# A Mamba block between two ternary FFNs on one core: the first FFN of the chunks as a stream of its own

## The chip, the core and the metric

The kernel runs on one core of a Trainium2 chip. The metric is the device time in microseconds (us) of one execution. The core has five engines that work side by side, each with its own instruction queue, which it works through in order: TensorE (PE, matrix products; its weight loads are listed as PEld), VectorE (DVE), ScalarE (ACT), GpSimd (POOL) and SyncE (SP, which issues most of the DMA transfers).

## The reference

The input x is 4096 rows (time steps) of 1024 numbers, in float32. Three residual blocks follow each other:

```
x = x + 0.5 * ffn(layernorm(x))
x = x + mamba(layernorm(x))
x = x + 0.5 * ffn(layernorm(x))

ffn(x)   = x @ w.T * scale + bias       # w: the weight rounded to -1, 0, 1; both FFNs share it
mamba(x): u, z = x @ W_in.T             # 1024 columns each
          u  = silu(conv_b + 4-tap convolution of u in time)
          dt_r, B, C = u @ W_xproj.T    # 64, 16, 16 columns
          dt = softplus(dt_r @ W_dt.T + b_dt)
          h_t = exp(dt_t * A) * h_(t-1) + dt_t * B_t * u_t     # 16 states for each column
          y  = sum over the 16 states of h_t * C_t  +  u * Dskip
          return (y * silu(z)) @ W_out.T
```

The recurrence runs over all 4096 time steps, so its 16 states are carried from one piece of the input to the next.

## The kernel before

**Tiling.** The rows are cut into 16 chunks of 256 time steps (`NC` = 16, `T` = 256), each chunk into two tiles of 128 rows (`TT`). The columns lie on partitions, in 8 blocks of 128, and a chunk's recurrence runs in two halves of 4 blocks. So there are 32 half-chunks, each with 16 states.

**The stages of a chunk**, with the lines to look for in the profile:

- First FFN ("a"): statistics of the rows on ACT and POOL (`stats`, L393 to L407), normalizing on ACT (`normed`, L412), transposes on PE (L428), each transposed group cut into a high part by ACT (L456) and a low part by DVE (L458), products with the ternary weight on PE (L499: 64 for a chunk; for chunk 0 L530, as the weight's blocks come), bias added by a DMA from POOL's queue (L472), residual on DVE (L479).
- Norm and u: the same statistics and transposes again, copies by ACT (L585), products with the u half of `w_in` on PE (L616), first tap of the convolution on ACT (L550), three more on DVE (L560), silu on ACT (L566).
- `steps`: the products with `w_xp` (L640), copies (L645, L648), B and C written to DRAM and read back spread over all partitions (`bc`, by `fetch`), the dt products (L708) and softplus on ACT (L720).
- `gates`: the products with the z half of `w_in` (L675), copied by ACT (L689), silu (L694).
- Recurrence, for each half and each of the 16 states: ACT makes the decays (L913, four pieces for two scans), POOL the entering term h = u * B (L934, with a small addition of the carried state, L941), DVE two scans (L966), then the product with C (L981); PE sums the states by transposed products with an identity (L1019). For three of the 16 states (`PAIRED`) DVE adds two products first (L996).
- Gate with z on DVE (L1036), transposes (L750) and copies (L740), products with `w_out` on PE (L758), residual on DVE (L729), then the second FFN ("c"), which uses the same lines as the first, and the store.

**What sets the order.** No engine chooses at run time. While the program is built, a planner (`Streams`, with a cost for each operation written at each `yield`) plays the streams through and writes the instructions into one fixed order for each engine. A stream is a generator: it yields either what it wants next (an engine, a duration, an earliest time) or a condition to wait for, such as `when("z", c, 1)`. Of those that could start first, the one with the lowest rank goes; the ranks are the constants `DECAY, ENTER, ...` and `FFN_A, NORM, U_PART, ...`, and a stream may change its rank by yielding a number. So a wait in the source is a wait in the plan: it moves instructions in the queues, and is no instruction itself. The streams around the change are `front` (first FFN, norm and u, chunk after chunk), `gates` (z of a chunk, spawned by `front` when its u products are recorded), `back` (`w_out` and the second FFN), and those of the recurrence. How far a stream may get ahead is limited by the buffers: 7 row tiles `xs`, 2 `xts`, 2 each of `his` and `los`, 5 weight buffers, 4 `us`, 3 PSUM banks and 3 PSUM banks for decays.

Of the kernel before, what the change touches and what calls it, by code (L numbers as in the profile page):

```python
# [53 lines left out]
REACH = 160  # L54
ISSUE, ADDED = 950, 6000
SWITCH = 1300

LATE_P, LATE_X, LATE_D, LATE_N = 300, 300, 1200, 300
PAIRED = (0, 4, 8)

DECAY, ENTER, SUM, PREPARE, RECUR, GATE = 4, 3, 1, 0, 5, 0
FFN_A, NORM, U_PART, CONV, DELTA, OUT, FFN_C = 1, 1, 3, 2, 2, 2, 3

HOLD = 250, 0, 0, 500
Z = 2, 4


class Streams:
# [109 lines left out]
def macaron_mamba_kernel(  # L178
# [16 lines left out]
    NC = S // T  # L195
# [84 lines left out]
    ready = {}  # L280

    def when(*key):
        return (yield lambda: ready.get(key, INF))
# [60 lines left out]
    def streamed(load, n, ahead, rank):  # L344

        queue = []

        def fill():
            for i in range(n):
                yield lambda: 0 if len(queue) < ahead else INF  # L350
                w = yield from weights.take()
                load(i, w)
                queue.append((order.now + 5000, w))

        order.spawn(fill(), rank)
        return queue
# [209 lines left out]
            nc.scalar.activation(flat(u[c, half]), flat(u[c, half]), AF.Silu)  # L566
            ready["u", c, half] = end + REACH

    def front():
        for c in range(NC):  # L570
            yield FFN_A
            at = [3500, 5000]
            for t in range(TT if c else 0):
                x_tiles[c, t] = yield from xs.take()
                load_x(c, t)
                at[t] = order.now + 5000
            ends = yield from ffn(c, "a", FFN_A, at)
            yield NORM
            queue = streamed(u_weights, NB, 2, U_PART)
            ln, rows_, at = yield from stats(c, ends)  # L580
            xT = yield from xts.take()

            def keep(g, pt, at_):
                end = yield act(512, at_)
                nc.scalar.copy(  # L585
                    xT[:, 4 * g : 4 * g + 4, PAD + t * P : PAD + (t + 1) * P],
                    pt.rearrange("p (j q) -> p j q", q=P),
                )
                banks.put(pt, end)
                ends.append(end + REACH)  # L590

            xns = []
            for t in range(TT):
                xns.append((yield from normed(c, ln, rows_, t, at)))
            lns.put(ln, xns[-1][1])
            ends = []
            for t in range(TT):
                xn, at = xns[t]
                yield from transposed(xn, at, keep, NORM)
                while len(ends) < 2 * (t + 1):  # L600
                    yield lambda: ends[2 * t + 1] if len(ends) > 2 * t + 1 else INF

            end = yield pool(190)
            nc.gpsimd.tensor_copy(xT[:, :, PAD - KER + 1 : PAD], halo)
            at = max(end, ends[-1]) + REACH
            yield U_PART
            for blk in range(NB):
                if blk % HB == 0:
                    u[c, blk // HB] = yield from us.take()
                pp = yield from banks.take()  # L610
                w = yield from arrived(queue)
                wt = w.rearrange("p (k m) -> p k m", m=P)
                for k in range(NB):
                    if k % 4 == 0:
                        end = yield pe(8 * (KER - 1 + T) * FULL, at)
                    nc.tensor.matmul(  # L616
                        pp[:, : KER - 1 + T],
                        wt[:, k, :],
                        xT[:, k, PAD - KER + 1 : PAD + T],
                        start=(k == 0),  # L620
                        stop=(k == NB - 1),
                    )
                order.spawn(conv(c, blk, pp, end + REACH), CONV)
                weights.put(w, end)
                if blk == 0:
                    yield pool(190, at)
                    nc.gpsimd.tensor_copy(halo, xT[:, :, PAD + T - KER + 1 : PAD + T])
            order.spawn(gates(c, xT), Z[0])
            order.spawn(steps(c), DELTA)
# [27 lines left out]
        xds.put(xd[c], order.now + 2000)  # L657

    def gates(c, xT):
        queue = streamed(z_weights, NB, 2, Z[0])  # L660
        for half in range(2):
            yield Z[half]
            sz[c, half] = yield from szs.take()
            for b in range(0, HB, 2):
                pp = yield from banks.take()
                pp = pp.rearrange("p (t j) -> p t j", t=TT)
                for part_ in range(2):
                    w = yield from arrived(queue)
                    wt = w.rearrange("p (j k m) -> p j k m", j=2, m=P)
                    for t in range(TT):  # L670
                        end = yield pe(8 * T * FULL)
                        for i in range(HB):
                            k = part_ * HB + i

                            nc.tensor.matmul(  # L675
                                pp[:, t, :],
                                xT[:, k, PAD + t * P : PAD + (t + 1) * P],
                                wt[:, :, i, :],
                                start=(k == 0 and t == 0),
                                stop=(k == NB - 1),  # L680
                                skip_group_check=True,
                            )
                    weights.put(w, end)
                order.spawn(kept(c, half, b, pp, end + REACH), Z[half])
        xts.put(xT, end)
# [86 lines left out]
    def back():  # L772
        for c in range(NC - 1):
            yield OUT
            yT = []
            for half in range(2):
                if half:
                    yield from when("product", c, 1, 0)
                    queue = streamed(lambda i, w: out_weights(i // 2, i % 2, w), NB, 3, OUT)
                yT.append((yield from us.take()))  # L780
                yield from turned(c, half, yT[half])
            for q in range(D // QW):
                po = yield from banks.take()
                po = po.rearrange("p (t j) -> p t j", t=TT)
                for half in range(2):
                    w = yield from arrived(queue)
                    for t in range(TT):
                        end = yield pe(8 * QW * FULL)
                        by_w_out(po, yT[half], w, half, t)
                    weights.put(w, end)  # L790
                for t in range(TT):
                    order.spawn(mixed(c, q, t, po, end + REACH + LATE_X), OUT)
            for half in range(2):
                us.put(yT[half], end)
            for q in range(D // QW):
                end = yield from when("mixed", c, q, 1)
            yield FFN_C
            ends = yield from ffn(c, "c", FFN_C, [end, end])
            for t in range(TT):
                yield from give_out(c, t, slice(0, D), ends[t])  # L800
                xs.put(x_tiles.pop((c, t)), order.now + 0)
        yield from last(NC - 1)
# [74 lines left out]
    def fetch():  # L877
        for c, half, n in items:
            if n < 0:
                continue  # L880
            yield from when("bc", c)
            bc = yield from bcs.take()
            nc.sync.dma_start(
                flat(bc),
                bc_dram[c][n : n + 1].rearrange("o a b -> o (a b)").to_broadcast([P, 2 * T]),
            )
            coming[c, half, n] = bc
            ready["come", c, half, n] = order.now + 3000

    def skipping():  # L890
        for i, (c, half) in enumerate(halves):
# [33 lines left out]
    def enter():  # L925
        for c, half, n in items:
            if n < 0:
                continue
            yield from when("g", c, half)
            yield from when("come", c, half, n)  # L930
            bc = coming[c, half, n]
            h = yield from hs.take()
            end = yield pool(2300, 0, True)
            nc.gpsimd.tensor_tensor(  # L934
                h, u[c, half], bc[:, 0:1, :].to_broadcast([P, HB, T]), ALU.mult
            )
            if n + 1 == NST:
                us.put(u[c, half], end)
            yield from when("over", c, half)
            end = yield pool(140, 0, True)  # L940
            nc.gpsimd.tensor_tensor(h[:, :, 0], h[:, :, 0], over[c, half][:, :, n], ALU.add)  # L941
            entering[c, half, n] = h
            ready["enter", c, half, n] = end + REACH
            if n + 1 == NST:
                overs.put(over[c, half], end)

# [93 lines left out]
    for rank, gen in (  # L1040
        (0, ternary()),
        (0, halved()),
        (0, fetch()),
        (FFN_A, front()),
        (OUT, back()),
        (PREPARE, prepare()),
        (DECAY, decaying()),
# [72 lines left out]
```

## Time and profile before

| | us |
|---|---|
| median of 3 runs | 2622.4 (2619.84 to 2623.95) |
| the profiled execution | 2623.95 |
| its span, first to last instruction | 2622.2 |
| PE busy | 2473.1 |
| DVE busy | 2467.7 |
| ACT busy | 1953.2 |
| POOL busy | 1746.9 |
| DVE, scans (L966), 1024 of them | 1215.5 |
| DVE, products with C (L981), 512 | 694.0 |
| DVE, sums of two products (L996), 96 | 193.4 |
| first scan of chunk 0 starts at | 102.06 |
| first scan of chunk 1, of chunk 2, of chunk 3 | 268.31, 424.08, 579.1 |

The mean granted TensorE clock of the profiled execution is 0.98. A line of the timeline gives the start, the time from the first to the last end, the engine, the line and the operation, then the tile written, the tiles read and how many instructions were merged; in brackets the engine's idle time in front and what ended it. A float32 product on PE (such as L616, L675, L758) shows as two records.

### The profile page before, as it was taken

What the parts mean: (1) busy time and instruction counts of PE and PEld (TensorE: products, weight loads), DVE (VectorE), ACT (ScalarE), POOL (GpSimd) and SP (SyncE); (2) the same over time, 40 slices, a digit from 0 to 9 for tenths busy, and PEclk for the clock granted to TensorE, in tenths of its full rate; (3) what the DMA queues carried; (4) which work ended last, traced back from release to release, by engine and by line L of the source; (5) the groups of instructions that cost most, each with busy time, mean ns of one, the idle gap of its engine ahead of it and who ended that gap; (6) DMA issues with size and microseconds to landing.
All of it is one profiled execution on the core that took longest, in us unless ns stands there. A gap on an engine that the chain in (4) does not pass through costs nothing. (4 is left out here: it accounts for less than half of the span.)

```text
span 2622.2 us, 38817 instructions
## 1 busy us (share of the span) xinstructions
PE 2473.1 (94%) x13314; PEld 2118.7 (81%) x13314; DVE 2467.7 (94%) x2532; ACT 1953.2 (74%) x4084; POOL 1746.9 (67%) x1433
## 2 busy tenths in 40 slices
PE   5987999999999999999999999999999999999867
PEld 4776778888888888888888888888888888888756
DVE  5589999999999999999999999999999999999994
ACT  3678678787778878777797878779787887876652
POOL 0456767767676776767677676766767677776772
PEclk9999899999999999999999999999999999999988
DMA  5544445556544555555555544555654455554451
GB/s 166 156 134 129 149 128 174 158 176 181 165 150 141 177 165 176 160 169 151 156 164 181 173 152 153 160 166 163 188 165 146 141 175 159 177 175 151 122 156 37
DMA packets 218541, 410.68 MB, mean 157 GB/s; under 512 B 19172, under 2 KB 85860, under 8 KB 218344
## 3 DMA queue, kind: packets, MB, share of 16 engines
q1 hardware_dynamic: 209128, 374.65, 44.2%
q0 software_dynamic: 9216, 33.56, 6.9%
q8 instruction: 105, 1.72, 0.3%
q14 instruction: 92, 0.75, 0.1%
HBM read 390.82 MB, written 17.31 MB: 156 GB/s over the span
## 5 line engine op out<-in xcount | busy, mean ns | idle before, releaser
L934 POOL TENSOR_TENSOR h<-u,bc 128x1024 f32<-128x1024 f32 x512 | 1224.2, 2391 | 565.8 <-ACT da L913 257.7
L913 ACT ACTIVATE da<-dt,pr 128x255 f32<-128x255 f32 x2048 | 946.3, 474 | 432.1 <-DVE h L966 398.9
L966 DVE TENSOR_TENSOR_SCAN h<-da,h 128x512 f32<-128x512 f32 x1024 | 1215.5, 1206 | 31.8 <-ACT da L913 22.3
L981 DVE TENSOR_TENSOR p<-h,bc 128x1024 f32<-128x1024 f32 x512 | 694.0, 1355 | 0.1
L1019 PE MATMUL y<-ident,p 128*128 128x128 f32 x3584 | 480.7, 279 | 74.2 <-DVE p L981 59.9
L1019 PEld LDWEIGHTS y<-ident,p 128*128 128x128 f32 x3584 | 423.0, 144 | 136.8 <-DVE p L981 81.1
L616 PE MATMUL bank<-xT,weight 128*128 128x259 f32 x2048 | 477.4, 386 | 11.1 <-issue 7.6
L675 PE MATMUL bank<-weight,xT 128*128 128x256 f32 x2048 | 478.0, 382 | 2.9 <-DMA weight<-in_w_in 1.0
L758 PE MATMUL bank<-weight,u 128*128 128x256 f32 x2016 | 464.1, 380 | 2.9 <-DMA weight<-in_w_out 2.8
L616 PEld LDWEIGHTS bank<-xT,weight 128*128 128x128 f32 x2048 | 384.0, 192 | 73.5 <-issue 10.8
L675 PEld LDWEIGHTS bank<-weight,xT 128*128 128x128 f32 x2048 | 377.5, 191 | 51.8 <-DVE x L479 2.9
L758 PEld LDWEIGHTS bank<-weight,u 128*128 128x128 f32 x2016 | 373.9, 191 | 49.5 <-ACT da L913 2.5
L941 POOL TENSOR_TENSOR h<-h,over 128x4 f32<-128x4 f32 x512 | 343.0, 670 | 33.7
L499 PE MATMUL bank<-wf,lo 128*128 128x512 f32 x976 | 255.7, 404 | 3.8 <-DVE lo L458 3.7
L499 PE MATMUL bank<-wf,hi 128*128 128x512 f32 x976 | 244.7, 393 | 0.0
L499 PEld LDWEIGHTS bank<-wf,lo 128*128 128x128 f32 x976 | 181.1, 190 | 44.3 <-DVE lo L458 8.0
L560 DVE SCALAR_TENSOR_TENSOR u<-bank,pr,u 128x256 f32<-128x256 f32 x384 | 176.4, 467 | 38.7 <-ACT u L550 36.4
L499 PEld LDWEIGHTS bank<-wf,hi 128*128 128x128 f32 x976 | 181.5, 188 | 37.2 <-issue 0.3
L996 DVE TENSOR_TENSOR p<-p,p 128x1024 f32<-128x1024 f32 x96 | 193.4, 2014 | 0.0
L395 POOL TENSOR_SCALAR ln<-ln 128x1 f32<-128x1 f32 x96 | 35.8, 373 | 182.0 <-ACT tmp L393 178.7
L428 PE MATMUL bank<-ident,tmp 128*128 128x128 f32 x756 | 114.5, 285 | 33.1 <-ACT tmp L412 24.0
L428 PEld LDWEIGHTS bank<-ident,tmp 128*128 128x128 f32 x756 | 93.1, 146 | 52.8 <-ACT tmp L412 30.2
(98 smaller groups left out, 1966.5 us busy)
## 6 DMA issues: line engine op xcount, KB each, us to landing
bc<-bcd SPq DMA_DIRECT2D x512, 256.0 KB, 3.7
weight<-in_w_in SPq DMA_DIRECT2D x128, 512.0 KB, 4.6
weight<-in_w_in SPq DMA_DIRECT2D x256, 256.0 KB, 5.6
weight<-in_w_out SPq DMA_DIRECT2D x128, 512.0 KB, 4.1
x<-hbias POOLq DMA_DIRECT2D x64, 512.0 KB, 9.4
x<-in_x SPq DMA_DIRECT2D x32, 512.0 KB, 5.0
out<-x SPq DMA_DIRECT2D x30, 512.0 KB, 4.5
weight<-in_w_ffn SPq DMA_DIRECT2D x5, 512.0 KB, 7.2
```

Source lines behind the costliest of these rows:

```text
L428: nc.tensor.matmul(pt[:, j * P : (j + 1) * P], xn[:, k * P : (k + 1) * P], ident, start=(j == 0), stop=(j == 3), is_transpose=True, skip_g ...
L499: nc.tensor.matmul(pf, x[:, k, :], wf[:, k, cols], start=(x is lo and k == 0), stop=(x is hi and k == NB - 1),)
L616: nc.tensor.matmul(pp[:, : KER - 1 + T], wt[:, k, :], xT[:, k, PAD - KER + 1 : PAD + T], start=(k == 0), stop=(k == NB - 1),)
L675: nc.tensor.matmul(pp[:, t, :], xT[:, k, PAD + t * P : PAD + (t + 1) * P], wt[:, :, i, :], start=(k == 0 and t == 0), stop=(k == NB - 1), ...
L758: nc.tensor.matmul(po[:, t, :], yT[:, b, t * P : (t + 1) * P], wt[:, b, :], start=(half == 0 and t == 0 and b == 0), stop=(half == 1 and b ...
L913: nc.scalar.activation(da[:, i, 1:], dt[c, half][:, b, 1:], AF.Exp, scale=a_neg[:, half * HB + b, n : n + 1],)
L934: nc.gpsimd.tensor_tensor(h, u[c, half], bc[:, 0:1, :].to_broadcast([P, HB, T]), ALU.mult)
L941: nc.gpsimd.tensor_tensor(h[:, :, 0], h[:, :, 0], over[c, half][:, :, n], ALU.add)
L966: nc.vector.tensor_tensor_scan(rows_, flat(da), rows_, 0.0, ALU.mult, ALU.add)
L981: nc.vector.tensor_tensor(p, h, bc[:, 1:2, :].to_broadcast([P, HB, T]), ALU.mult)
L996: nc.vector.tensor_tensor(flat(p), flat(p), flat(q), ALU.add)
L1019: nc.tensor.matmul(y[t][:, b * P : (b + 1) * P], p[:, b, t * P : (t + 1) * P], ident, start=(first and b == 0), stop=(n == NST - 1 and b = ...
```

## The change

The first FFN leaves `front` and becomes a stream of its own, `first_ffns`, which keeps the rank `FFN_A` and goes from chunk to chunk as far as the buffers let it; `front` starts with rank `NORM` and waits for the FFN of its chunk. `front` takes its `xT` buffer ahead of the statistics and not behind them. `gates` waits in the plan until the z of the chunk in front is done (its half 1). Besides, some constants of the plan change: the rank of z's second half (4 to 5), the due time of a streamed weight (5000 to 3500 ns behind its issue), the moment from which the `w_out` loads of a chunk are issued (state 0 of half 1 to state 12), the due time of a broadcast B and C (3000 to 4000 ns), and 300 ns are added to the plan's due time of an entering term (`LATE_E`). The operations and their number are the same; the order on each engine is a new one.

```diff
-LATE_P, LATE_X, LATE_D, LATE_N = 300, 300, 1200, 300
+LATE_P, LATE_X, LATE_D, LATE_E, LATE_N = 300, 300, 1200, 300, 300
...
-Z = 2, 4
+Z = 2, 5
...
-                queue.append((order.now + 5000, w))
+                queue.append((order.now + 3500, w))
...
-    def front():
+    first = {}
+
+    def first_ffns():
         for c in range(NC):
-            yield FFN_A
             at = [3500, 5000]
             for t in range(TT if c else 0):
                 x_tiles[c, t] = yield from xs.take()
                 load_x(c, t)
                 at[t] = order.now + 5000
-            ends = yield from ffn(c, "a", FFN_A, at)
+            first[c] = yield from ffn(c, "a", FFN_A, at)
+            ready["ffn", c] = order.now
+
+    def front():
+        for c in range(NC):
             yield NORM
+            yield from when("ffn", c)
+            ends = first[c]
             queue = streamed(u_weights, NB, 2, U_PART)
+            xT = yield from xts.take()
             ln, rows_, at = yield from stats(c, ends)
-            xT = yield from xts.take()
...
     def gates(c, xT):
+        if c:
+            yield from when("z", c - 1, 1)
         queue = streamed(z_weights, NB, 2, Z[0])
...
-                    yield from when("product", c, 1, 0)
+                    yield from when("product", c, 1, 12)
...
-            ready["come", c, half, n] = order.now + 3000
+            ready["come", c, half, n] = order.now + 4000
...
-            ready["enter", c, half, n] = end + REACH
+            ready["enter", c, half, n] = end + REACH + LATE_E
...
-        (FFN_A, front()),
+        (FFN_A, first_ffns()),
+        (NORM, front()),
```

## The prediction

> **What bounds the kernel now.** First I read the page's totals and its forty slices:
>
> ```profile
> PE 2473.1 (94%) x13314; PEld 2118.7 (81%) x13314; DVE 2467.7 (94%) x2532; ACT 1953.2 (74%) x4084; POOL 1746.9 (67%) x1433
> ...
> DVE   5589999999999999999999999999999999999994
> ```
>
> VectorE (DVE) and TensorE (PE) are both full, except at the two ends. To see which of them sets the pace I cut the span at the first scan (L966) of chunks 0, 1, 2 and 3 (102.06, 268.31, 424.08 and 579.10 us in DVE's timeline) and asked for busy times by stretch; the columns are start:end, length, PE, PEld, DVE, ACT, POOL, PE clock, DMA share, GB/s:
>
> ```profile
> 0.00:102.06 102.06, 69.60 (x304) 57.74 (x305) 44.81 (x73) 47.56 (x77) 13.63 (x32) 0.93 0.52 168
> 102.06:268.31 166.25, 140.01 (x724) 118.14 (x722) 144.43 (x141) 130.61 (x264) 105.25 (x89) 0.91 0.43 128
> 268.31:424.08 155.77, 148.05 (x787) 126.69 (x788) 149.81 (x154) 112.32 (x239) 105.27 (x83) 0.96 0.54 162
> 424.08:579.10 155.02, 151.96 (x833) 130.60 (x833) 152.64 (x157) 121.64 (x256) 108.38 (x90) 1.00 0.54 164
> ```
>
> From chunk 2 on a chunk takes 155.0 us, DVE idles 2.4 of them and PE 3.1: DVE sets the pace. What is lost lies before the first scan (DVE idle 57.2 of 102.1 us), in chunk 0 (21.8) and in chunk 1 (6.0). DVE's waits, asked for chunk 0 and for chunk 1, begin with one line each (who waits for whom, us in total, times, longest):
>
> ```profile
> DVE h L966 <- ACT da L913: 11.3, 7, 6.3
> ...
> DVE h L966 <- POOL h L934: 4.1, 1, 4.1
> ```
>
> Scans wait for ScalarE's decays (ACT, L913), once for 6.3 us, and once for POOL's entering term (L934). So the total is: time of the first scan, plus DVE's remaining work, plus DVE's idle time after it.
>
> **What the change moves.** I compared the order of the instructions of both built programs, engine by engine. From the first scan of chunk 2 to that of chunk 14, DVE's and POOL's orders are the same, instruction for instruction; on PE and ACT one small group per chunk changes places (four transposed products L1019 behind eight products L758; one copy L689 behind two exponentials), and some loads on SP's queue. So the first FFN does not run ahead in the steady part any more than before. The change is chunks 0 and 1, and a little of chunk 15.
>
> **Part 1, the first scan.** PE gets, ahead of chunk 0's dt products (L708): the FFNs of chunks 1 and 2 (each 64 products at 8 in 1.82 us, 14.5, and 16 transposes L428 at 4 in 0.44, 1.8), chunk 1's norm transposes (1.8) and 16 more products for z (7.1 by "86.40 7.07 L675 x32", where one product is two records). Sum 41.5 us. Some of it falls into a gap of PE:
>
> ```profile
> 39.47 0.39 PE L530 MATMUL y<-wf,hi 128*128 128x512 f32 x1
> 48.72 3.67 PE L428 MATMUL bank<-ident,tmp 128*128 128x128 f32 x16 [8.87 <-ACT tmp L412]
> ```
>
> Chunk 1's transposes start at 39.8, its hi/lo chain (ACT 0.58, DVE 0.69 per group) lets the products start at 42.6; they end at 57.1. Chunk 0's norm transposes stand behind them; 2.7 us with their copies, so u (L616) starts at 59.8 instead of 52.26: +7.5. Into u go chunk 2's 16.3 us, and I add 1.2 for the hand-overs of the three PSUM banks; behind u stand 8.9 us of z and norm products more than before, of which 1.6 replace PE's wait for the silu at 84.59. L708 ends at 126.9 instead of 94.5 (+32.4). Behind it ACT now also has z's silu with its table (1.28 + 1.06), and DVE has six taps of chunk 1's convolution that wait for u's second block on PE: first scan at **136.8** instead of 102.1, **+34.7 us**. Bounds: 131.3, if PE never stalls (39.9 us plus 83.9 of ordered work gives 123.8, and the old 7.5 from L708's end to the scan); 139, if ACT holds up two of the convolutions by its L393/L397 of 1.0 to 1.2 each.
>
> A page speaks against this step. The Trainium skill, "ScalarE: Activation LUTs", section "What ACT_TABLE_LOAD costs", puts every switch at about 2.66 us, 1.28 of load and 1.38 of drain. In this trace the load takes 1.28 and the next activation starts 1.29 behind it (127.67, 128.97), with no drain of that size; with the page's figure the three switches ahead of the first scan would add an estimated 4.1 us, and I go by the row.
>
> **Part 2, what DVE has done by then.** Ahead of the first scan now stand 8 more L479 (0.66 apart: 5.3), 4 more L458 (0.61: 2.4) and 6 taps L560 (0.49: 2.9): **-10.7 us** that chunk 0 need not do. Net at this point: +24.0.
>
> **Part 3, chunk 0.** 21.8 us of its 166.25 were idle time of DVE, which the earlier work on PE may save. But chunk 0 is now barer. A step is two scans and a product (L981). Where nothing else of DVE lies in it, it looks so, in the tail of before:
>
> ```profile
> 2558.65 2.32 DVE L966 TENSOR_TENSOR_SCAN h<-da,h 128x512 f32<-128x512 f32 x2
> 2560.90 1.39 DVE L981 TENSOR_TENSOR p<-h,bc 128x1024 f32<-128x1024 f32 x1
> 2562.22 2.32 DVE L966 TENSOR_TENSOR_SCAN h<-da,h 128x512 f32<-128x512 f32 x2
> 2564.47 1.40 DVE L981 TENSOR_TENSOR p<-h,bc 128x1024 f32<-128x1024 f32 x1
> ```
>
> L981 takes 1.40 instead of 1.19, and the step 3.57 instead of 3.37 (2 x 1.125 + 1.12): POOL's L934 of 2.35 is running. A bare step with a pairwise sum (L996, 2.50 there, 1.20 at its best) takes 6.0 to 6.6. The order has 20 bare plain steps in chunk 0 (13 before) and 4 bare ones with a sum (1 before). So chunk 0 is 20 x 3.57 + 6 x 3.37 + 4 x 6.1 + 2 x 4.9 + 12.3 of other work = 138.1 us, without stalls.
>
> Stalls: the 10.5 us of ACT work (table loads, dt, z's silu, two norms) that stood ahead of scan 13's decay and cost DVE 6.3 is broken up, since chunk 1's norm now comes before the first scan. But the order has new clumps: 8.8 us of ACT work ahead of scan 38 against 7.6 us of DVE work in the three scans that the three decay buffers cover, 8.7 ahead of scan 46 against 6.6, and three of 3.7 to 4.2 ahead of scans 8, 12 and 16, in bare steps. I put 3, 3.5 and together 2.5, and 1 for the rest: 10 us (bounds: 2, if the buffers cover all but the difference; 16, if each costs like scan 13's, about 6 for each large clump). Chunk 0 takes **148** instead of 166.25: -18.2. Chunk 1 then starts at 284.8 instead of 268.3: **+16.5**.
>
> **Part 4, chunk 1.** Its DVE work is the same; the clump ahead of its first scan shrinks from 8.7 to 5.8 us, so I halve the 4.1 us wait for POOL: **-1.8** (bounds -4.5, nothing of its idle time above the steady part's is left; 0).
>
> **Part 5, the rest.** z's wait for the z of the chunk in front, the later start of the w_out loads (product 12 instead of 0) and the new due times are waits of the planner, not of an engine: they add no semaphore and show only in the orders compared above. Behind a displaced L675 or L758 on PE stands the next L1019, for which DVE waits only at a chunk's two gates (L1036, 0.2 us there); behind a displaced load on SP stand broadcasts for POOL (bc, 3.7 us to land, six buffers ahead). Steady chunks: 0 (bounds: 0.3 us each way in 13 chunks, 4 in all, since the displaced L689 is 0.5 long and DVE's named waits in a chunk are 0.7 and less). The SP loads (w_in and w_out, landing in 4.1 to 5.6 us) are hidden by the queue of two or three weights; without that cover each would cost PE about the 1.0 to 2.3 us it waited for weights in the tail, not DVE. The tail has the same DVE work: 0.
>
> **Sum**: the first scan +34.7, chunk 0 -18.2 (10.7 of it the moved work), chunk 1 -1.8: 34.7 - 18.2 - 1.8 = **+14.7 us**. The profiled execution took 2623.95 (span 2622.2), which would become 2638.7; the median, 2622.4, becomes **2637**.
>
> **Rivals.**
> *The start is made good* (13%). PE stalls nowhere (131.3), chunk 0 has 2 us of stalls (140.1) and chunk 1 loses nothing (-4.5): 29.2 - 26.2 - 4.5 = -1.5, so 2621; it decides from 9.5 us of these 16 on. For it: in the steady part the planner's order leaves DVE only 2.4 us idle in 155. Against: chunks 0 and 1 together held 27.8 us of idle time, and the first scan alone, less the moved work, costs 24.0 of them.
> *Chunk 0 starves* (17%). The clumps on ACT cost like scan 13's, 16 us, the bare steps run at 3.7, and the start takes 139: 14.7 + 6 + 2.6 + 2.2 = +25.5, 2648.
> *Faster* (4%): the displaced group in every chunk removes DVE's steady idle time. It is 2.4 us a chunk, at most 13 x 2.4 = 31, giving 2606; it decides from (14.7 + 5.2) / 13 = 1.5 us a chunk on. The named waits there (L479 for PE 0.7, L966 for ACT 0.7) hardly reach that.
>
> **Numbers.** The forecast, +6 to +22, has 66%. Runs of this kernel can tell about 0.2%, 5.2 us, from no change. Slower: 66 + 17 = 83%; same: 13%; faster: 4%. That the FFN does not run ahead after chunk 2 is no rival, but read from the order and part of the forecast. The range leaves out the last rival and half of the first below, and the worst of the starving case above: 2625 to 2648.
>
> **What would show it.** Right: first scan near 137; L479 of chunks 1 and 2 before it; chunk 0 near 148 with L981 at 1.40; steady chunks at 155.0. Wrong: a first scan before 131, chunk 0 above 156 or below 140, or a steady chunk off 155.0 by over 0.3.

## The result, and the profile after

The changed kernel takes **2641.3 us** (median of 3 runs, 2639.08 to 2641.84) where the kernel before takes 2622.4: a ratio of 1.0071, 95% interval 1.0048 to 1.0094. The forecast was 2637, range 2625 to 2648, slower with 83%. The profiled execution has a span of 2639.5 us instead of 2622.2, so 17.3 us have to be found.

The page's totals and DVE's forty slices of the kernel after:

```profile
PE 2476.7 (94%) x13314; PEld 2119.4 (80%) x13314; DVE 2473.8 (94%) x2532; ACT 1951.1 (74%) x4082; POOL 1754.1 (66%) x1433
...
DVE  5298999999999999999999999999999999999994
```

The totals hardly differ from those of before (ScalarE's two instructions fewer are table loads, 189 instead of 191), and the slices differ only near the start: 5589 became 5298. Most of the loss arises there, and totals over the whole span hide it. The same cut as before, at the first scan of each of the first chunks (start:end, length, then busy time of PE, PEld, DVE, ACT and POOL, PE's granted clock, DMA share, GB/s):

```profile
0.00:134.64 134.64, 114.29 (x533) 95.23 (x534) 56.13 (x92) 70.10 (x113) 23.97 (x47) 1.00 0.55 173
134.64:282.55 147.91, 99.41 (x494) 82.80 (x492) 134.11 (x125) 108.04 (x230) 103.02 (x74) 0.77 0.33 107
282.55:438.10 155.55, 146.13 (x787) 125.16 (x788) 153.45 (x155) 110.48 (x235) 108.13 (x84) 0.98 0.53 158
438.10:593.42 155.32, 152.15 (x833) 130.63 (x832) 152.94 (x157) 121.33 (x256) 108.47 (x90) 1.00 0.54 164
```

The first scan comes at 134.64 instead of 102.06. By then DVE has done 56.1 us of work instead of 44.8, and PE 114.3 instead of 69.6. Chunk 0 is shorter, 147.91 instead of 166.25, and from chunk 1 on the two kernels keep the same pace. The whole sum, from the scans' start times in both traces:

| stretch | before | after | difference |
|---|---|---|---|
| start to the first scan | 102.06 | 134.64 | +32.6 |
| chunk 0 | 166.25 | 147.91 | -18.3 |
| chunk 1 | 155.77 | 155.55 | -0.2 |
| chunks 2 to 13, each | 155.07 | 155.18 | +0.1 (12 of them +1.4) |
| chunk 14 | 151.79 | 151.67 | -0.1 |
| chunk 15, first half | 74.87 | 76.83 | +2.0 |
| from there to the end | 110.6 | 110.7 | +0.1 |
| sum | 2622.2 | 2639.5 | +17.3 (the differences, rounded one by one, give 17.5) |

What PE did ahead of the first scan stands in its timeline (in brackets: PE's idle time in front, and what ended it):

```profile
43.04 2.11 PE L499 MATMUL bank<-wf,lo 128*128 128x512 f32 x8
...
57.70 2.16 PE L428 MATMUL bank<-ident,tmp 128*128 128x128 f32 x16
60.15 10.72 PE L623 MATMUL bank<-xT,weight 128*128 128x259 f32 x48 [0.28 <-issue]
...
123.98 1.14 PE L717 MATMUL bank<-xd,wd 64*128 64x256 f32 x8
```

(L623 is u's product and L717 dt's; most lines lie 7 to 9 further down than before.) Chunk 1's FFN runs from 43.04 to 57.70 in front of u, which starts at 60.15. The first dt products end at 125.1; before, they ended at 94.5. Between these two lines PE idles 0.1 us: it isn't waiting, and part of what it does is work that nobody needs yet.

DVE's waits in chunk 0, and the longest in chunk 1:

```profile
DVE h L975 <- ACT da L922: 9.6, 2, 5.3
DVE h L975 <- POOL h L950: 3.0, 1, 3.0
...
DVE h L975 <- POOL h L950: 3.9, 3, 3.0
```

In chunk 0 two waits for decays are left of seven. DVE's timeline puts them at the 38th scan (4.26 us) and the 46th (5.29), the two clumps that the prediction named (scans counted from 0). The wait of 3.0 for POOL stands in both lists: it is the one in front of chunk 1's first scan, and by time it lies in chunk 0's stretch.

### The profile page after: what moved, and what is told of

Same layout as the page of the kernel before. It is cut to its first block, busy times and chain, and to the rows that moved or that the text cites. A ratio compares the mean times of both kernels' runs of the same rounds, so it can differ in the third digit from the quotient of the medians.

```text
span 2639.5 us, 38859 instructions
## 1 busy us (share of the span) xinstructions
PE 2476.7 (94%) x13314; PEld 2119.4 (80%) x13314; DVE 2473.8 (94%) x2532; ACT 1951.1 (74%) x4082; POOL 1754.1 (66%) x1433
## 5 line engine op out<-in xcount | busy, mean ns | idle before, releaser
L1028 PE MATMUL y<-ident,p 128*128 128x128 f32 x3584 | 488.5, 282 | 97.8 <-DVE p L990 67.3
L1028 PEld LDWEIGHTS y<-ident,p 128*128 128x128 f32 x3584 | 428.7, 146 | 162.9 <-DVE p L990 91.6
L623 PE MATMUL bank<-xT,weight 128*128 128x259 f32 x2048 | 474.4, 384 | 8.7 <-issue 7.8
L623 PEld LDWEIGHTS bank<-xT,weight 128*128 128x128 f32 x2048 | 381.6, 190 | 69.5 <-issue 11.0
L950 POOL TENSOR_TENSOR h<-h,over 128x4 f32<-128x4 f32 x512 | 354.2, 692 | 34.5
L499 PEld LDWEIGHTS bank<-wf,lo 128*128 128x128 f32 x976 | 180.2, 189 | 44.8 <-DVE lo L458 7.1
L1005 DVE TENSOR_TENSOR p<-p,p 128x1024 f32<-128x1024 f32 x96 | 199.2, 2075 | 0.0
L395 POOL TENSOR_SCALAR ln<-ln 128x1 f32<-128x1 f32 x96 | 32.6, 340 | 174.7 <-ACT tmp L393 173.8
L479 DVE SCALAR_TENSOR_TENSOR x<-bank,hscl,x 128x512 f32<-128x512 f32 x124 | 91.4, 737 | 39.0 <-PE bank L499 38.1
```

The source lines that it names most:

```text
L499: nc.tensor.matmul(pf, x[:, k, :], wf[:, k, cols], start=(x is lo and k == 0), stop=(x is hi and k == NB - 1),)
L623: nc.tensor.matmul(pp[:, : KER - 1 + T], wt[:, k, :], xT[:, k, PAD - KER + 1 : PAD + T], start=(k == 0), stop=(k == NB - 1),)
L1005: nc.vector.tensor_tensor(flat(p), flat(p), flat(q), ALU.add)
L1028: nc.tensor.matmul(y[t][:, b * P : (b + 1) * P], p[:, b, t * P : (t + 1) * P], ident, start=(first and b == 0), stop=(n == NST - 1 and b = ...
```

## The experiments

The theory: the total changes by what the first scan is later, less the work that DVE has done by then, less the idle time saved in chunk 0; and the first scan is set by what stands on PE ahead of chunk 0's dt products. Rivals: the new order costs time in the chunks themselves; or one of the constants is what costs. One table for all runs, so that only what is special need be told later. Times are of the scans in each trace; "last half" is the first half of chunk 15; the ratio is to the kernel before on the same chip.

| run | first scan | chunk 0 | chunks 2 to 13, each | last half | median | ratio (95%) |
|---|---|---|---|---|---|---|
| before | 102.1 | 166.3 | 155.07 | 74.9 | 2622.4 | |
| after | 134.6 | 147.9 | 155.18 | 76.8 | 2641.3 | 1.0071 (1.0048, 1.0094) |
| e1, most FFN products of chunks 1, 2 out | 120.9 | 148.1 | 155.22 | 77.1 | 2628.4 | 1.0026 (1.0015, 1.0037) |
| e2, no stream, new constants | 134.8 | 157.1 | 155.02 | 76.8 | 2649.4 | 1.0106 (1.0091, 1.0121) |
| e3, stream, old constants | 155.8 | 147.7 | 155.14 | 75.5 | 2663.0 | 1.0159 (1.0144, 1.0174) |
| e4, chunk 2's FFN held | 118.4 | 155.1 | 155.20 | 76.9 | 2631.1 | 1.0038 (1.0023, 1.0053) |
| e5, due time alone | 134.8 | 159.3 | 169.6 | 77.4 | 2842.7 | 1.0849 (1.0828, 1.0871) |
| e6, other constants | 102.5 | 166.7 | 155.15 | 75.5 | 2627.4 | 1.0018 (1.0008, 1.0027) |
| e7, stream held with its loads | 102.1 | 163.6 | 164.0 | 74.8 | 2737.8 | 1.0438 (1.0420, 1.0455) |
| e8, z held too | 97.6 | 172.8 | 164.4 | 75.3 | 2746.1 | 1.0475 (1.0460, 1.0491) |
| e9, due time and product 12 | 135.4 | 157.3 | 155.10 | 76.4 | 2652.6 | 1.0118 (1.0104, 1.0132) |
| e10, held but loaded | 105.1 | 173.9 | 155.10 | 74.9 | 2633.8 | 1.0049 (1.0035, 1.0063) |
| e11, z held alone | 102.3 | 170.8 | 155.05 | 74.9 | 2630.4 | 1.0033 (1.0021, 1.0046) |
| e12, held past the first scans | 97.5 | 167.9 | 155.02 | 75.9 | 2621.3 | 0.9999 (0.9990, 1.0008) |

### Taking PE's work away

**e1** (on after):

```diff
-                    for k in range(NB):
+                    few = key in (("a", 1), ("a", 2))
+                    for k in (0 if x is lo else NB - 1,) if few else range(NB):
```

> Of the changed kernel's first FFNs of chunks 1 and 2, 112 of 128 products are left out on PE (only the first and the last of each group of 16 are kept, so the FFN's values for these two chunks are not the reference's); every engine's order is otherwise that of the changed kernel. THEORY (PE's work ahead of chunk 0's dt products is what delays the first scan): 112 x 0.227 = 25.4 us less PE work; chunk 0's normed rows are ready only near 51.8, so u starts near 54 instead of 60.2, the second FFN gives another 12.7: first scan near 116 instead of 134.6, chunk 0 unchanged at 148 (its stalls are ACT's), total about 2621 to 2623, all of the loss gone. RIVAL (the new order in chunk 0, with its bare steps and clumps on ACT, is what costs, and the first scan would only shift slack): total stays within 5 us of 2641.

13.7 us came off the first scan, not 18.6, and nearly the same off the end (span 2626.2, 13.3 less), while chunk 0 stayed at 148.1. So some two thirds of the loss went, not all of it. PE's timeline of this run shows where the rest stayed:

```profile
50.80 3.68 PE L428 MATMUL bank<-ident,tmp 128*128 128x128 f32 x16 [3.58 <-ACT tmp L412]
54.34 1.99 PE L624 MATMUL bank<-xT,weight 128*128 128x259 f32 x7
...
77.88 0.47 PE L500 MATMUL bank<-wf,lo 128*128 128x512 f32 x1 [2.55 <-DVE u L561]
```

Without the products PE waits 3.58 us for ScalarE's normalizing (L412), and u starts at 54.34 as expected. What was not expected lies behind that. Chunk 2's missing products give 9.3 us instead of 12.7, since PE now waits for DVE's convolution (2.55 us at 77.88), and u's second block takes 11.9 us (79.28 to 91.16, granted clock 0.88) instead of 10.5 (clock 1.00). So the FFN had covered such waits, and its price at the start is less than its length. The products with `w_xp` then start 13.7 us earlier (91.16 instead of 104.87), and so does the first scan: PE's path to the dt products sets it.

**e4** (on after) leaves all work in and moves half of it:

```diff
     def first_ffns():
         for c in range(NC):
+            if c == 2:
+                yield from when("dt", 0, 0)
```

> The changed kernel, with one more wait in the plan: the stream's FFN of chunk 2 waits for chunk 0's first dt. PE's ordered work up to the dt products falls from 100.4 to 84.2 us. THEORY: first scan near 118.4 instead of 134.6, DVE has 5.1 us less done ahead, chunk 0 takes about 151 to 153 instead of 148; total about 2628 to 2631, a half to two thirds of the loss gone. RIVAL (the order in chunk 0 costs): within 5 us of 2641.

The first scan came at 118.4, as expected. Chunk 0 took 155.1 instead of 147.9, since what DVE no longer does ahead of the first scan it does there, and a little more than expected. Of 16.2 us gained at the start, 7.2 are given back in chunk 0; in the whole change it is 18.3 of 32.6.

### The stream and the constants, apart

**e2** undoes the stream and keeps the rest, **e3** does the stream alone:

```diff
e2, on after:
-            first[c] = yield from ffn(c, "a", FFN_A, at)
-            ready["ffn", c] = order.now
-
-    def front():
-        for c in range(NC):
+            ends = yield from ffn(c, "a", FFN_A, at)
             yield NORM
-            yield from when("ffn", c)
-            ends = first[c]
...
-        (FFN_A, first_ffns()),
-        (NORM, front()),
+        (FFN_A, front()),
e3, on before (with the reverse of the first part):
-        (FFN_A, front()),
+        (FFN_A, first_ffns()),
+        (NORM, front()),
```

> The changed constants and z's wait stay, but the first FFN goes back into front, as before. THEORY that the stream alone delays the start: total 2622, first scan 102. By this program's order, however, the constants alone already put chunk 1's FFN and 12 more z products ahead of chunk 0's dt products, 26.9 us of PE work more than before: then the first scan is near 127, DVE has 2.7 us done ahead, chunk 0 saves some 10 us of its idle time, total about 2634. RIVAL (the constants are neutral): 2622.

> The kernel before with the new stream alone: old constants, no wait of z. By its order PE has 120.3 us of work to chunk 0's dt products, 19.9 more than the changed kernel (chunk 1's u has come ahead as well). THEORY (PE's ordered work up to the dt products sets the first scan): first scan near 154, DVE 2.9 us further ahead, total about 2641 + 17 - 3 = 2653 to 2657. RIVAL (the stream is what the chunk can absorb, the constants make the loss): 2622 to 2630.

Neither part alone is as cheap as the two together: the constants (with z's wait) cost 28 us, the stream 42, both 19. e3 met its number (PE has 120 us of ordered work ahead of the dt products there, after 100). e2 missed: 134.8 and not 127, though PE's dt products ended at 119.87. From there to the first scan e2 has this stretch, columns as above:

```profile
119.87:134.83 14.96, 13.71 (x69) 10.83 (x68) 1.23 (x1) 14.84 (x25) 9.85 (x13) 1.00 0.31 105
```

ScalarE is busy 14.84 of 14.96 us: two L397, an L393 and two L412 of later norms, and three table loads, stand in its queue between the first softplus and the decay that the first scan waits for (DVE idles 8.81 us for it). So there is a **second bound** on the first scan, ScalarE's work behind the dt products. In before that stretch is 7.56 us long (7.48 busy), in after 9.54 (9.38 busy); the prediction had put 9.9 for it.

**e5** takes the due time alone, **e6** the constants without it (both on before, with the `xT` buffer taken earlier, which by itself moves no instruction):

```diff
e5:
-                queue.append((order.now + 5000, w))
+                queue.append((order.now + 3500, w))
e6:
-Z = 2, 4
+Z = 2, 5
...
-                    yield from when("product", c, 1, 0)
+                    yield from when("product", c, 1, 12)
...
-            ready["come", c, half, n] = order.now + 3000
+            ready["come", c, half, n] = order.now + 4000
...
-            ready["enter", c, half, n] = end + REACH
+            ready["enter", c, half, n] = end + REACH + LATE_E
```

> The kernel before with one constant changed: a streamed weight is due 3500 ns behind its issue instead of 5000. No stream of its own, all else as before. The theory (the order ahead of chunk 0's dt products on PE sets the first scan, and this constant alone already puts chunk 1's first FFN there): first scan near 134.8 us as in the run with the old front and all new constants, chunk 0 near 157, the last half-chunk near 76.8 us instead of 74.9, in all 2646 to 2652. The rival (a due time only shifts loads and is neutral; the constants mattered by something else): first scan near 102, 2622 within 4.

> The kernel before with the other four constants of the change (rank of z's second half 5, w_out loads from product 12 on, B and C due at 4000, 300 ns on an entering term), without the due time of 3500, without the stream and without z's wait. The theory: PE has as much work ahead of chunk 0's dt products as before (59 us), so the first scan is near 102 us, chunk 0 near 166, the last half-chunk near 75, in all 2622 within 5. The rival (these constants carry a part of the loss): 2630 or more, or a gain of 5 and more if they are what was good in the change.

e6 comes out at 1.0018 of before, its median 0.4 us outside what was expected. Its scans are 0.4 us late at the first one and 2.1 us at the last, a little in many stages: these constants carry nothing of the change's start, neither loss nor gain. Its ten times fall into two groups, 2621.9 to 2623.3 and 2627.4 to 2628.0, and the trace is of the upper one; what parts them was not found. e5's first scan is where the theory puts it, and its total is not: 2843, worse by 190 us than any expectation. It lies in every chunk. One steady chunk of e5, and DVE's three largest waits in it:

```profile
1043.89:1213.00 169.11, 157.64 (x830) 132.93 (x830) 147.26 (x156) 120.84 (x254) 105.83 (x88) 0.97 0.50 149
```

```profile
DVE h L966 <- ACT da L913: 7.3, 1, 7.3
DVE h L966 <- POOL xT L604: 5.6, 1, 5.6
DVE u L560 <- ACT u L550: 2.7, 1, 2.7
```

DVE idles 21.8 of 169.1 us, in single long waits, where before it idles 2.4. The instructions are the same; their order is another one, and it stays so from chunk 2 on, where DVE's and POOL's orders are those of before in all runs with 155 us a chunk. Two theories were open: the weights come too late with a due time of 3500 (then every kernel with it would lose), or the plan has tipped into another repeating order. The kernel after itself speaks for the second, and **e9** decides it, with one more constant on e5:

```diff
-                    yield from when("product", c, 1, 0)
+                    yield from when("product", c, 1, 12)
```

> As the run with the due time of 3500 alone (2842.7, 169 us a chunk in the steady part), with one constant more: the w_out loads of a chunk wait for product 12 of half 1 instead of product 0. The theory (the plan settles into one of several repeating orders; with loads due at 3500 the early w_out loads tip it into a bad one, and the later ones give before's order of DVE and POOL back): steady chunks at 155.0 to 155.3, first scan 134.8, chunk 0 near 157, last half-chunk 76.8, in all 2648 (2643 to 2653). The rival (the due time itself makes the weights come too late and costs DVE's idle time in each chunk, whatever the w_out loads do): steady chunks at 165 or more, 2790 or more in all.

```profile
1069.31:1224.34 155.03, 152.00 (x833) 130.60 (x832) 152.65 (x158) 121.62 (x256) 108.37 (x90) 1.00 0.55 164
```

The steady chunk is back at 155.03, DVE's and POOL's orders are again those of before, and the total is 2652.6 (4.6 above the number, within the range). So "product 12", which costs and gains next to nothing among the constants of e6, is worth 14.5 us in each chunk beside the due time of 3500: it decides which order the plan settles into. The first half of chunk 15 takes 76.4 to 77.4 us in every run with a due time of 3500 and 74.8 to 75.9 in every run with 5000, with or without the stream. DVE's and POOL's orders there are those of after in all runs with 3500, and in none with 5000; so most of the +2.0 us there goes with this constant, though e12 shows 1.0 of it without.

### Holding the early work back

If early work costs on PE, it should be held until chunk 0's dt products are out. **e7** (on after, due time 5000) and **e8** (z held as well):

```diff
e7:
         for c in range(NC):
+            if c in (1, 2):
+                yield from when("dt", c - 1, 0)
             at = [3500, 5000]
e8, besides:
         if c:
             yield from when("z", c - 1, 1)
+        else:
+            yield from when("dt", 0, 0)
         queue = streamed(z_weights, NB, 2, Z[0])
```

> The kernel after with the due time back at 5000 and the stream of the first FFN held, for chunks 1 and 2 alone, until the first dt product of the chunk in front is recorded. The theory: PE has 59 us of work ahead of chunk 0's dt products as in before, so the first scan is at 100 to 103 us; chunk 0 has a clump of 10.5 us of ACT work ahead of its fourth scan, so 164 to 168; the last half-chunk 75; in all 2616 to 2624. The rival (the stream costs time in the chunks themselves, not by the first scan): first scan near 102, but 2630 or more in all.

> As the run with the held stream, and chunk 0's z products wait too until the first dt product of chunk 0 is recorded, which takes 7 us of PE's work from ahead of the dt products (52 us there). The theory: first scan near 96.5 us (B and C, fetched by DMA, then bound it), chunk 0 near 157 since the clumps of ACT's work in it are 5 us at most, chunk 1 and the steady chunks as in before, last half-chunk near 75: about 2607 in all (2603 to 2618), faster than both kernels. The rival (what is taken from ahead of the first scan comes back as waits in chunk 0): first scan near 97, chunk 0 at 170 or more, 2620 or more in all.

The first scans came as expected, 102.1 and 97.6, and the totals were 116 and 125 us above before: the second surprise of this kind. Chunks 2 to 13 take 164 us each, and the order of DVE from chunk 2 on is a third one. Its two largest waits in one such chunk of e7:

```profile
DVE lo L458 <- ACT hi L456: 3.4, 1, 3.4
DVE x L479 <- PE bank L499: 3.1, 1, 3.1
```

The first one, followed back through the timeline of ACT, POOL and DVE:

```profile
1214.43 1.06 ACT L393 ACTIVATE tmp<-x 128x1024 f32<-128x1024 f32 x1 [2.70 <-DMA x<-in_x]
...
1219.65 2.37 ACT L412 ACTIVATE tmp<-x,ln 128x1024 f32<-128x1024 f32 x2 [1.06 <-POOL ln L407]
...
1222.42 0.57 ACT L456 CAST hi<-bank 128x512 fp32r<-128x512 f32 x1
...
1223.03 0.69 DVE L458 TENSOR_TENSOR lo<-bank,hi 128x512 fp32r<-128x512 f32 x1 [3.42 <-ACT hi L456]
```

The rows of x land late for this place in the order, the statistics, the normalizing, the transposes and the cast follow one behind the other, and DVE's L458 stands in front of a scan: 3.42 us of this chain come out as DVE's idle time. In chunk 0 of e8 the held loads are waited for directly:

```profile
101.55 13.54 PE L688 MATMUL bank<-weight,xT 128*128 128x256 f32 x48 [9.56 <-DMA weight<-in_w_in]
111.68 0.59 ACT L702 COPY sz<-bank 128x512 f32<-128x512 f32 x1 [7.05 <-PE bank L688]
112.74 1.22 DVE L979 TENSOR_TENSOR_SCAN h<-da,h 128x512 f32<-128x512 f32 x1 [10.69 <-ACT da L926]
```

z's products wait 9.56 us for weights that could have been there, ScalarE stands 7.05 us behind z's copy, and DVE 10.69 us behind the decays queued after that copy. **e10** keeps the waits and puts them behind the loads (on e8):

```diff
         for c in range(NC):
-            if c in (1, 2):
-                yield from when("dt", c - 1, 0)
             at = [3500, 5000]
             for t in range(TT if c else 0):
                 x_tiles[c, t] = yield from xs.take()
                 load_x(c, t)
                 at[t] = order.now + 5000
+            if c in (1, 2):
+                yield from when("dt", c - 1, 0)
             first[c] = yield from ffn(c, "a", FFN_A, at)
...
+        queue = streamed(z_weights, NB, 2, Z[0])
         if c == 0:
             yield from when("dt", 0, 0)
-        queue = streamed(z_weights, NB, 2, Z[0])
```

and **e11** makes the second of these edits alone, on the kernel before.

> The run with the stream and z held (2746.1), with the two waits put behind the loads: the rows of x for chunks 1 and 2 and the first two z weights of chunk 0 are loaded as in after, and only the products wait in the plan for the first dt product of the chunk in front. The theory (what went wrong there was that the loads were held along, so that ScalarE stood 7 us behind z's products in chunk 0, and that the plan fell into another order afterwards): first scan 98 to 101 (ScalarE has 4.8 us of statistics more ahead of the first decay than there), steady chunks 155.0 to 155.3, last half-chunk 75; chunk 0 near 162 (4 for a clump of 6.0 us of ACT work at its second scan, 6 for one of 13.0 at chunk 1's first scan, some 6 elsewhere); in all 2615 (2608 to 2622). The rival (what is held back costs in chunk 0 what the early first scan gains): first scan near 99, chunk 0 at 168 or more, 2622 or more in all.

> The kernel before, with one change: the z products of chunk 0 wait in the plan, behind their loads, until the first dt product of chunk 0 is recorded; no stream, all constants as before. PE's ordered work ahead of that product is 52.0 us instead of 59.1. The theory: first scan 97 to 100 instead of 102.1, chunk 0 near 167 (its clumps of ACT work are 8.3 and 4.7 us in place of one of 10.5, the one at chunk 1's first scan 8.7 as before), all later chunks as before, in all 2619 (2614 to 2623). The rival (the first scan is bound by something else): first scan at 102, 2622.

e10 confirms one half: with the loads early the steady chunks are at 155.10 again, DVE's and POOL's orders there are those of before, and the total is 112 us below that of e8. Chunk 0 itself gained nothing by the early loads (173.9 instead of 172.8); what came back lies in the later chunks, where both the loads and the order differ, and no run takes these two apart. The other half fell in both runs. The first scans were 105.1 and 102.3, not 98 to 101 and 97 to 100, and chunk 0 took 173.9 and 170.8. e10's chunk 0 and e11's first scan are the rivals' numbers, and both totals lie above what the theory said. The stretch from the end of the first dt products to the first scan, e10 and then e11:

```profile
89.60:105.05 15.45, 13.28 (x63) 11.16 (x63) 1.23 (x1) 15.36 (x27) 11.77 (x15) 1.00 0.78 272
```

```profile
92.40:102.32 9.92, 7.67 (x34) 6.17 (x33) 3.83 (x5) 9.49 (x18) 4.99 (x7) 0.66 0.97 262
```

ScalarE is busy 15.36 of 15.45 and 9.49 of 9.92 us. PE was through earlier than in before, and ScalarE filled the time with chunk 1's statistics and normalizing, ahead of the first decay in e10 and among the softplus in e11. In e10 it is e2's second bound again: the first scan waits 12.53 us for a decay. In e11 ScalarE's work comes in by a detour: DVE's L862 (dt times u) stands behind two hi/lo cuts that wait for ScalarE, POOL's entering term behind L862, and the first scan waits 0.87 us for that term. **e12** moves that work too (on e10, without the 300 ns on an entering term and without the wait of chunk 2):

```diff
-            if c in (1, 2):
-                yield from when("dt", c - 1, 0)
+            if c in (1,):
+                yield from when("product", c - 1, 0, 2)
...
-            yield from when("dt", 0, 0)
+            yield from when("product", 0, 0, 0)
```

> As the run that is held but loaded (2633.8; first scan 105.1, chunk 0 173.9), with later conditions: chunk 1's first FFN waits in the plan for chunk 0's third product with C, chunk 0's z for its first one, chunk 2's FFN for nothing, and the 300 ns on an entering term are left off. In the two runs before, PE was through with the dt products at 89.6 and 92.4 us, and ScalarE then worked 15.4 and 9.5 us on end, chunk 1's statistics and normalizing among it, until the first scan. The theory (below 59 us of ordered PE work, ScalarE's work between the dt products and the first decay bounds the first scan): with that work behind the first scans, the first scan is at 97 to 98.5, as where the stream's loads were held too (97.6). ScalarE's clumps in chunk 0 are 7.5, 5.3, 3.6, 4.1 and 6.5 us, and 8.7 and 4.2 at chunk 1's first scan, so chunk 0 takes 165 to 169; steady chunks 155.0, last half 75; in all 2615 to 2621. The rival (PE's and DMA's work bounds it): first scan at 102 or later, 2622 or more in all.

ScalarE's timeline of e12, from the first softplus to the decays of the first scan:

```profile
90.74 1.28 ACT L926 ACT_TABLE_LOAD   x1
92.03 0.48 ACT L926 ACTIVATE da<-dt,pr 128x255 f32<-128x255 f32 x1
...
95.58 1.28 ACT L926 ACT_TABLE_LOAD   x1
96.88 3.19 ACT L926 ACTIVATE da<-dt,pr 128x255 f32<-128x255 f32 x7
```

The first scan comes at 97.46, as the theory has it: with PE's and ScalarE's work ahead of it moved, it comes earlier. ScalarE still sets it. The scan needs two decays, and between the first (92.03) and the second (96.88) stand the softplus of the other half and two table loads, while POOL's entering term is done at 95.67. It is the same in e8 (second decay at 97.00, scan at 97.58), where B and C had been expected to bound it. The total is 2621.3, equal to before (0.9999, 0.9990 to 1.0008). Of 4.6 us gained at the start, 1.6 are given back in chunk 0, 1.0 in the first half of chunk 15 and 1.1 behind it; the span ends 1.7 us earlier than that of before, too little to be told from nothing. No run beat the kernel before by a measurable amount.

## Why the prediction was right, point by point

**The sum.** The forecast was +14.7 us, and the spans differ by 17.3. The first scan came 2.2 us earlier than forecast, chunk 0 as forecast, chunk 1 gave 1.6 less, and 3.4 came up where nothing had been put.

**Part 1, the first scan.** Forecast 136.8, measured 134.64. u started at 60.15 (59.8 forecast), the dt products ended at 125.1 (126.9), and the last stretch took 9.5 us (9.9). e1 and e4 show that this work sets the scan's time: taken out or held back, it gave 13.7 and 16.2 us. The prediction counted the stretch behind the dt products correctly for this order: ScalarE is busy in 9.38 of the 9.54 us, and the last 2.7 of them are DVE's six convolution taps, which had waited for ScalarE. It did not say how this stretch grows when more of ScalarE's work lands in it, and so the expectations for e2, e10 and e11 were too early by 2 to 8 us.

**The page on table loads.** The Trainium skill, "ScalarE: Activation LUTs", "What ACT_TABLE_LOAD costs", puts a drain of about 1.38 us on each switch beside the 1.28 us load. After's trace agrees with the row that was taken: the load at 124.69 takes 1.28 us and the softplus starts 1.29 us behind its start. It holds for nearly every switch of the trace: 185 of 188 loads have the next activation 1.29 to 1.32 us behind their start, and all 188 start less than 0.1 us behind the end of the one in front. The load is there; no drain of that size shows.

**Part 2, work done ahead.** 10.7 us forecast; DVE's busy time ahead of the first scan rose by 56.13 - 44.81 = 11.3.

**Part 3, chunk 0.** Forecast 148, measured 147.91, but its two terms were each off. The work was put at 138.1 and was 134.11. The product with C does take 1.40 us in a bare step, as read from the tail of before, but in 16 steps instead of 20 (0.8 us; the mean is 1302 ns). The last of the 32 products falls behind chunk 1's first scan (1.1 us), and the other work, put at 12.3 by its full lengths, took 10.9, since one instruction starts a little ahead of the end of the one in front. The stalls were put at 10 and were 13.8: the large clumps cost 4.26 and 5.29 (3 and 3.5 forecast), the small ones at scans 8, 12 and 16 nothing (2.5 forecast), and a wait of 3.0 for POOL at chunk 1's first scan was not in this sum but in part 4's. Two errors of 4 us cancel, which is luck.

**Part 4, chunk 1.** Forecast -1.8, measured -0.2. The reason given was wrong: the 4.1 us wait for POOL ends at chunk 1's first scan, so it lies in chunk 0's stretch of before and is part of the 21.8 us there. It fell to 3.0, not to a half. Chunk 1's own idle time fell from 6.0 to 2.1 us by other waits (for the first tap L550 from 2.8 to 0.3, for the `w_out` products from 1.4 to nothing). But DVE's busy time rose by 3.6: the product with C takes 1375 ns instead of 1312 (32 of them, 2.0 us) and the sum of two products 2279 instead of 1995 (6, 1.7 us). The traces show why:

```profile
291.01 2.36 POOL L943 TENSOR_TENSOR h<-u,bc 128x1024 f32<-128x1024 f32 x1 [2.35 <-ACT da L922]
...
291.93 2.52 DVE L1005 TENSOR_TENSOR p<-p,p 128x1024 f32<-128x1024 f32 x1
```

A product or sum of DVE that starts while POOL's product runs ends 1.08 us behind POOL's end (here 294.45 behind 293.37), in both traces, with a spread from 1.08 to 1.21; one that starts at another time takes 1.20. In chunk 1, 19 of these 38 instructions of DVE start inside a product of POOL, where 14 did in before.

**Part 5, the rest.** Forecast 0; measured +1.4 in twelve steady chunks (inside the bounds of 4) and +2.0 in the last half-chunk, which was not foreseen. The tail was called the same because its work is the same; its order is not, and e5 and e9 tie that to the due time. Which instruction of the new order costs the 2 us was not settled.

**What the prediction got right without knowing why.** It read from the built orders that chunks 2 to 13 keep their order, and put 0 there. e5, e7 and e8 show how much hung on it: the same kind of edit, with one constant or one wait elsewhere, cost 9 to 14.5 us in each chunk. z's wait in `gates`, the rank of z's second half and the due time of B and C move no instruction on any engine when they are taken out of the kernel after: the built orders are the same, so they are without effect there. Why the plan falls into one order and not another was not traced inside the planner.

**The rivals.** "The start is made good" needed a first scan near 131 and chunk 0 at 140: neither came. "Chunk 0 starves" needed 16 us of stalls, a first scan at 139 and a chunk 0 near 157. "Faster" needed a steady chunk 1.5 us shorter: it is 0.1 longer. The two parts of the change do not add: the due time moves chunk 1's FFN ahead of chunk 0's dt products even without the stream (e2, e5, e9), and with the stream the constants make the start 21 us earlier than the stream alone (134.6 and 155.8). By the built orders it is the due time again: of the constants it alone changes what PE does ahead of these products.

## What to carry to other kernels

Running a stage ahead can help only where the bounding engine would otherwise wait for that stage. Here DVE waited for the first scan of all, and everything that ran ahead stood in front of it; of the delay, DVE makes good the work that it did meanwhile and the waits that it is spared later, here 18.3 of 32.6 us. When a plan fixes the order, compare the built orders over the whole program for every edit, the steady part first, for a constant that does nothing alone can decide, beside another, which repeating order results. And try to hold back work without its loads: in e7 and e8, where the wait was placed ahead of the loads, engines stood waiting for the DMA (2.70 and 9.56 us above). How much of the 112 us between e8 and e10 is owed to that, and how much to the order, is open.

## What the runs showed of the hardware

PE's granted clock fell in stretches where PE often stands idle: 0.77 in after's chunk 0, where PE is busy 99 of 148 us, and 0.66 in e11's stretch ahead of the first scan. The busy share alone doesn't fix it: chunk 0 of before had 0.91 at 84% busy, after's first 134.6 us 1.00 at 85%. What the low clock cost in chunk 0, where DVE sets the pace, no run isolates. In e1 it cost PE about what the ratio says: u's second block took 11.9 us at 0.88 and 10.5 at 1.00.

A product of VectorE that starts while one of GpSimd runs gets done only behind it. Of the 512 products with C in after, 206 start so, and they end 1.08 to 1.16 us behind GpSimd's end; the other 306 take 1.20 us at the median.

The same operations on the same engines take 170 or 155 us a chunk, 190 us in all, by their order (e5 and e9, which differ in one constant of the plan).
